# Starting the first scan of a Mamba layer: order of the first two pieces, dt in halves, input loads spread over the scans

## The chip, the cores and the metric

The kernel runs on one core of one Trainium2 chip. The metric is the device time of one execution in microseconds (us); the time before is the median of three runs. One execution was also recorded by the hardware profiler; all traces in this document are of such executions. Engines: PE does matrix products, ACT activation functions, DVE and POOL elementwise work (DVE also the scan instruction), SP issues the DMAs.

## The reference

Four layers run one after the other on an image of 2 x 256 x 48 x 48 floats. Only the first, a Mamba layer, is touched by the change. Per batch image it has 2304 tokens of 256 channels:

```
h   = layernorm(seq) + pos                       # pos: table of sines and cosines, scaled
xi, z = split(h @ in_proj.T)                     # 512 channels each
# for the forward direction, and once more with xi and z reversed in time:
xs  = silu(causal_conv4(xi) + conv_b)
dt, B, C = split(xs @ xproj.T)                   # 16, 16 and 16 columns
dt  = softplus(dt @ dtproj.T + dt_b)
state[t] = exp(dt[t] * A) * state[t-1] + dt[t] * xs[t] * B[t]     # 16 states a channel
y[t]  = sum_n state[t] * C[t] + D * xs[t]
out = seq + ((y_f * silu(z)) + (y_b * silu(z))) @ out_proj.T
```

The other layers (attention with a feed-forward part, a graph layer with experts, attention with a mixture of experts) follow and read what the first one left.

## The kernel before, in words

**Tiling.** Each image is cut into 6 pieces of W = 384 tokens. Channels lie on the 128 partitions: 256 channels are two blocks, the 512 inner channels DB = 4 blocks, so a whole tile of inner channels is 128 x 1536. The input x stays in SBUF as `xres` (L73) for the whole kernel. Every float32 matmul shows in the trace as two matmul instructions.

**Three kinds of work per piece**, each a Python generator that yields between its steps so that its instructions can be laid between those of another:

- `project_in(b, c)` (L213): load pos; layer norm through matmuls with a constant matrix (means L221, difference L222, square L224, variance L228, Sqrt L230, scalings of pos L232, reciprocal L236, products L238 and L240); then eight output blocks, L247 with copy L252, of which the first four (xi) go to DRAM at L254 and the last four (z) at L256. It has 12 steps: 4 of normalization, 8 of blocks.
- `prepare(b, s, c, got)` (L297): load the window xw of xi from DRAM (L302), convolution as matmuls with diagonal weights (L311, copies L315), Silu (L321), xproj (L327, L331; B and C go to DRAM, L333), then dt: four small matmuls (L341) with Abs and Relu (L344, L345), and softplus on whole 128 x 1536 tiles: Exp L347, plus one L350, Ln L352, minus one L353, three DVE steps L355 to L357, and on POOL dtu = dt * xs (L359).
- `scan(step, beside, ...)` (L499): for each of the 4 channel blocks and 16 states one decay (ACT, L544), one scan instruction (DVE, L550 forward, L553 backward) and one product with C (L558, on DVE or POOL), summed by PE (L512). POOL makes the inputs db of four states at a time (L527) from bb, which with cc is loaded from DRAM for each group of four states (L522, L524). Two states make a slot; a scan has 32.

**Order.** There are 24 scans: two images, two directions, six pieces. During scan i, `beside` holds the generators that are laid into its slots: `prepare` for scan i+1 (15 steps over 25 slots), and during the first ten scans `project_in` for pieces (0, 2) to (1, 5), one per scan (12 steps over 32 slots). Before the first scan, `project_in(0, 0)`, `project_in(0, 1)` and `prepare(0, "f", 0)` run one after the other in the Python text. The eleven loads of x beyond the first (L167) are issued ahead of all that, and the 1 MB weight w_in in one DMA (L199).

The Python order isn't the order on the chip. The framework places each instruction on its engine's queue by its own estimate of when it is ready: earlier text goes first, but a later instruction is taken forward where the estimate sees the engine idle. On the chip each engine then works its queue strictly in that order, SP's DMA issues included. The framework also inserts all waits. Buffers are shared by tag: `up` has one buffer per tag (h, sq, pos, rs, xw, ex, ln), `wp` two (xs, dt, dtu, xz, bb, cc, db); the tag ln also serves the backward scans' yf (L504). PSUM tiles come from `hold()` (L208): five buffers before the scans begin, one during them.

Of the kernel before, what the change touches and what calls it, by code (L numbers as in the profile page):

```python
# [18 lines left out]
F32 = mybir.dt.float32  # L19
I32 = mybir.dt.int32  # L20
BF16 = mybir.dt.bfloat16
AF = mybir.ActivationFunctionType
ALU = mybir.AluOpType
# [4 lines left out]
P = 128  # L28
NB, C, HH, WW = 2, 256, 48, 48
L = HH * WW  # L30
T = NB * L
NT = T // P
W = 384
NCH = L // W
# [64 lines left out]
def bc(ap, shape, axis):  # L99

    return ap.unsqueeze(axis).to_broadcast(shape)
# [60 lines left out]
    yield  # L162


def load_x(E, b, c):
    xin = E.p["x"].rearrange("b (k p) n -> p b k n", p=P)
    E.nc.sync.dma_start(  # L167
        E.xres[:, :, b * L + c * W : b * L + (c + 1) * W], xin[:, b, :, c * W : (c + 1) * W]
    )

# [1 line left out]
def layer0(ctx, E):  # L174
# [9 lines left out]
    nc, tc, p = E.nc, E.tc, E.p  # L184
    NS, DB = 16, 4
# [5 lines left out]
    wp = ctx.enter_context(tc.tile_pool(name="l0w", bufs=2))  # L191
    up = ctx.enter_context(tc.tile_pool(name="l0u", bufs=1))
    psh = ctx.enter_context(tc.tile_pool(name="l0ps_h", bufs=5, space=PSUM))
    ps = ctx.enter_context(tc.tile_pool(name="l0ps_s", bufs=1, space=PSUM))
    psy = ctx.enter_context(tc.tile_pool(name="l0ps_y", bufs=1, space=PSUM))

    load_x(E, 0, 0)
    w_in = big.tile([P, 2, 1024], F32, name="w_in")
    nc.sync.dma_start(w_in, p["in_proj_wT"].rearrange("(k p) m -> p k m", p=P))  # L199
    xi_d, z_d, yf_d = [], [], []  # L200
    edge = up.tile([P, DB, 3], F32, name="edge")
    nc.vector.memset(edge, 0.0)
# [5 lines left out]
    def hold():  # L208

        pool, tag = (ps, "mm") if scanning else (psh, "hs")  # L210
        return pool.tile([P, 512], F32, tag=tag, name="mm")[:, :W]

    def project_in(b, c):  # L213

        src = E.xres[:, :, b * L + c * W : b * L + (c + 1) * W]
        pos = up.tile([P, 2, W], F32, tag="pos", name="pos")
        nc.sync.dma_start(pos, p["pos"].rearrange("(k p) n -> p k n", p=P)[:, :, c * W : (c + 1) * W])
        h = up.tile([P, 2, W], F32, tag="h", name="h")
        mp = hold()
        for k in range(2):  # L220
            nc.tensor.matmul(mp, lhsT=E.mean_c, rhs=src[:, k, :], start=k == 0, stop=k == 1)  # L221
        nc.vector.tensor_tensor(h, src, bc(mp, [P, 2, W], 1), ALU.subtract)  # L222
        sq = up.tile([P, 2, W], F32, tag="sq", name="sq")
        nc.scalar.activation(sq, h, AF.Square)  # L224
        yield
        vp = hold()
        for k in range(2):
            nc.tensor.matmul(vp, lhsT=E.mean_c, rhs=sq[:, k, :], start=k == 0, stop=k == 1)  # L228
        rs = up.tile([P, 2 * C], F32, tag="rs", name="rs")[:, :W]
        nc.scalar.activation(rs, vp, AF.Sqrt, bias=E.eps[1e-5])  # L230
        for k in range(2):
            nc.scalar.activation(  # L232
                pos[:, k, :], pos[:, k, :], AF.Identity, bias=E.v("ln_b", k, 1), scale=E.v("pos_scale")
            )
        yield
        nc.vector.reciprocal(rs, rs)  # L236
        yield
        nc.vector.tensor_tensor(h, h, bc(rs, [P, 2, W], 1), ALU.mult)  # L238
        for k in range(2):
            nc.vector.scalar_tensor_tensor(  # L240
                h[:, k, :], h[:, k, :], E.v("ln_g", k, 1), pos[:, k, :], ALU.mult, ALU.add
            )
        yield
        for m in range(2 * DB):
            px = hold()
            for k in range(2):
                nc.tensor.matmul(  # L247
                    px, lhsT=w_in[:, k, m * P : (m + 1) * P], rhs=h[:, k, :],
                    start=k == 0, stop=k == 1,
                )  # L250
            xz = wp.tile([P, W], F32, tag="xz", name="xz")
            nc.scalar.copy(xz, px)  # L252
            if m < DB:
                nc.sync.dma_start(xi_d[b][:, m, 3 + c * W : 3 + (c + 1) * W], xz)  # L254
            else:
                nc.sync.dma_start(z_d[b][:, c, m - DB], xz)  # L256
            yield

    scanning = False
    first = project_in(0, 0)  # L260
    next(first)
    for b in range(NB):
        for c in range(NCH):
            if (b, c) != (0, 0):
                load_x(E, b, c)
        nc.sync.dma_start(xi_d[b][:, :, 0:3], edge)
        nc.sync.dma_start(xi_d[b][:, :, L + 3 : L + 6], edge)
    w_x, w_dt, nega, w_d = {}, {}, {}, {}
# [14 lines left out]
    one = big.tile([P, 2], F32, name="one")  # L283
# [10 lines left out]
            nc.scalar.activation(t[:, j, :], E.ident, AF.Copy, scale=E.v(f"conv_w_{s}", j, 1))  # L294
        return t

    def prepare(b, s, c, got):  # L297

        fwd = s == "f"
        t0 = c * W  # L300
        xw = up.tile([P, DB, W + 3], F32, tag="xw", name="xw")
        nc.sync.dma_start(xw, xi_d[b][:, :, t0 + (0 if fwd else 3) : t0 + W + (3 if fwd else 6)])  # L302
        if (b, s) not in w_cv:
            w_cv[b, s] = taps(s)
        yield
        xs = wp.tile([P, DB, W], F32, tag="xs", name="xs")
        for d in range(DB):
            px = hold()
            for k in range(4):
                o = k if fwd else 3 - k  # L310
                nc.tensor.matmul(  # L311
                    px, lhsT=w_cv[b, s][:, d * 4 + k, :], rhs=xw[:, d, o : o + W],
                    start=k == 0, stop=k == 3,
                )
            nc.scalar.activation(xs[:, d, :], px, AF.Identity, bias=E.v(f"conv_b_{s}", d, 1))  # L315
            if d == 0:
                y = wp.tile([P, DB, W], F32, tag="y", name="y")
                if not fwd:
                    nc.sync.dma_start(y, z_d[b][:, c])
            yield  # L320
        nc.scalar.activation(xs, xs, AF.Silu)  # L321
        if not fwd:
            nc.scalar.activation(y, y, AF.Silu)
        yield
        pj = hold()
        for d in range(DB):
            nc.tensor.matmul(  # L327
                pj[:48, :], lhsT=w_x[s][:, d, :], rhs=xs[:, d, :], start=d == 0, stop=d == DB - 1
            )
        pr = wp.tile([48, W], F32, tag="pr", name="pr")  # L330
        nc.scalar.copy(pr, pj[:48, :])  # L331
        bcd = dr.tile([48, W], F32, tag="bcd", name="bcd")
        nc.sync.dma_start(bcd[16:48, :], pr[16:48, :])  # L333
        yield


        dt = wp.tile([P, DB, W], F32, tag="dt", name="dt")
        ex = up.tile([P, DB, W], F32, tag="ex", name="ex")
        for d in range(DB):
            pd = hold()  # L340
            nc.tensor.matmul(  # L341
                pd, lhsT=w_dt[s][:, d * P : (d + 1) * P], rhs=pr[0:16, :], start=True, stop=True
            )
            nc.scalar.activation(ex[:, d, :], pd, AF.Abs, bias=E.v(f"dt_b_{s}", d, 1))  # L344
            nc.scalar.activation(dt[:, d, :], pd, AF.Relu, bias=E.v(f"dt_b_{s}", d, 1))  # L345
            yield
        nc.scalar.activation(ex, ex, AF.Exp, scale=-1.0)  # L347
        dtu = wp.tile([P, DB, W], F32, tag="dtu", name="dtu")
        ln = up.tile([P, DB, W], F32, tag="ln", name="ln")
        nc.scalar.activation(dtu, ex, AF.Identity, bias=one[:, 0:1])  # L350
        yield
        nc.scalar.activation(ln, dtu, AF.Ln)  # L352
        nc.scalar.activation(dtu, dtu, AF.Identity, bias=one[:, 1:2])  # L353
        yield
        nc.vector.tensor_tensor(ex, ex, dtu, ALU.subtract)  # L355
        nc.vector.tensor_tensor(dt, dt, ln, ALU.add)
        nc.vector.tensor_tensor(dt, dt, ex, ALU.add)  # L357
        yield
        nc.gpsimd.tensor_tensor(dtu, dt, xs, ALU.mult)  # L359
        got.extend((b, s, c, xs, y, dt, dtu, bcd))  # L360
        yield

    def project_out(b, c, y):

# [216 lines left out]
    order = [  # L581
        (b, s, i, i if s == "f" else NCH - 1 - i) for b in range(NB) for s in "fb" for i in range(NCH)
    ]
    for steps in (first, project_in(0, 1)):
        for _ in steps:
            pass
    ready = []
    for _ in prepare(0, "f", 0, ready):
        pass
    scanning = True  # L590
    pieces = [(0, c) for c in range(2, NCH)] + [(1, c) for c in range(NCH)]
    after = None
    heads = chain(head_products(), contexts())
    n_late = -(-(36 + 1 + 2 * 5 * NCH) // (len(order) - 1 - len(pieces)))
    for i, (b, s, step, c) in enumerate(order):
        now, ready = ready, []
        beside = [(after, 4, 8)] if after else []
        if i + 1 < len(order):
            nb, s2, _, c2 = order[i + 1]
            beside.append((prepare(nb, s2, c2, ready), 15, 25))  # L600
        if i < len(pieces):
            beside.append((project_in(*pieces[i]), 12, 32))
        elif len(pieces) <= i < len(order) - 1:

            beside.append((islice(heads, n_late), n_late, 32))
        if (b, s, step) == (1, "f", 1):

            beside.append((group_stats(E, up, lambda: hold()[:, 0:2], 0), 3, 20))
        scan(step, beside, *now)
        after = chain(project_out(b, c, now[4]), piece_stats(E, b, c)) if s == "b" else None  # L610
# [1522 lines left out]
```

## Time and profile before

| what | us |
|---|---|
| median of 3 runs (5334.69 to 5339.48) | 5338.1 |
| the profiled execution | 5298.49 |
| its span | 5296.7 |
| first matmul of the first piece's blocks (L247) | 20.14 |
| first scan instruction (L550) | 102.11 |
| last PE sums of the last scan (L512) begin | 2457.18 |
| DVE busy over the span | 3472.5 |
| POOL busy over the span | 2416.0 |
| ACT busy over the span | 2395.3 |
| PE busy over the span | 4765.0 |

A row of the timeline gives start, length, engine, line, operation, what is written from what, and in brackets how long the engine was idle before it and what released it. "SPq" is SP's queue: the time is that of issuing, not of the transfer. A busy PE is not a PE at its peak, since matmul ends are modelled.

### The profile page before, as it was taken

How to read it: one execution, taken by the hardware profiler on the slowest of the kernel's cores; microseconds unless marked ns; L12 is line 12 of the kernel's file. 1: busy time of each engine (PE TensorE's matmuls, PEld its weight loads, DVE VectorE, ACT ScalarE, POOL GpSimd, SP SyncE). 2: the span in 40 equal slices, each digit the busy share in tenths (PEclk: the TensorE clock that was granted, in tenths of full speed). 3: DMA queues.
4: the chain of work that ended last, by engine and by line, in shares of the span. 5: the costliest groups of instructions: out<-in, count | busy, mean ns of one | idle time of the engine just before them, and what ended most of it. 6: DMA issues, size and time to landing. Idle time of an engine off the chain costs nothing. (4 is left out here: it accounts for less than half of the span.)

```text
span 5296.7 us, 47498 instructions
## 1 busy us (share of the span) xinstructions
PE 4765.0 (90%) x15282; PEld 2642.2 (50%) x15282; DVE 3472.5 (66%) x5366; ACT 2395.3 (45%) x5021; POOL 2416.0 (46%) x1323
## 2 busy tenths in 40 slices
PE   7888888888888888877999999999999999999897
PEld 3444344444444434433555555556655555555676
DVE  4999988889888878889999544546724410211344
ACT  5767766765766766762222323422133222222221
POOL 2888887788888788886000000028612100000331
PEclk8999999999999999999999999999989999999898
DMA  4454454444544344443110000111121100000422
GB/s 155 167 173 172 169 177 159 167 173 165 173 150 161 138 162 152 162 152 135 36 44 32 6 16 1 38 33 28 19 96 48 48 3 9 7 9 6 85 84 97
DMA packets 187427, 504.63 MB, mean 95 GB/s; under 512 B 33591, under 2 KB 106683, under 8 KB 186908
## 3 DMA queue, kind: packets, MB, share of 16 engines
q1 hardware_dynamic: 178460, 488.74, 26.9%
q0 software_dynamic: 8704, 12.73, 1.6%
q8 instruction: 123, 2.02, 0.2%
q14 instruction: 140, 1.15, 0.1%
HBM read 425.88 MB, written 75.51 MB: 95 GB/s over the span
## 5 line engine op out<-in xcount | busy, mean ns | idle before, releaser
L512 PE MATMUL yp<-hc,ident 128*128 128x384 f32 x3072 | 1185.8, 517 | 206.3 <-DVE hc L558 166.1
L527 POOL TENSOR_TENSOR db<-dtu,bb 128x1536 f32<-128x1536 f32 x384 | 1322.9, 3445 | 53.5 <-DVE hs L553 13.5
L512 PEld LDWEIGHTS yp<-hc,ident 128*128 128x128 f32 x3072 | 573.4, 197 | 764.5 <-DVE hc L558 317.7
L558 POOL TENSOR_TENSOR hc<-ho,cc 128x384 f32<-128x384 f32 x576 | 587.9, 1028 | 243.6 <-DVE ho L553 103.1
L558 DVE TENSOR_TENSOR hc<-hs,cc 128x384 f32<-128x384 f32 x960 | 499.9, 538 | 82.5 <-PE yp L512 81.3
L544 ACT ACTIVATE hs<-dt,negab 128x384 f32<-128x384 f32 x768 | 435.2, 581 | 94.6 <-DVE hc L558 44.1
L544 ACT ACTIVATE hs<-dt,negaf 128x384 f32<-128x384 f32 x768 | 434.5, 581 | 67.3 <-DVE hc L558 32.6
L550 DVE TENSOR_TENSOR_SCAN hs<-hs,state,db 128x384 f32<-128x384 f32 x400 | 395.3, 1008 | 33.9 <-POOL db L527 21.5
L553 DVE TENSOR_TENSOR_SCAN hs<-hs,state,db 128x384 f32<-128x384 f32 x400 | 393.3, 1005 | 34.6 <-POOL db L527 16.1
L1938 POOL DMA_INDIRECT xe<-xt_d,token x48 | 47.4, 987 | 752.5 <-issue 713.1
L311 PE MATMUL mm<-xw,w_cv 128*128 128x384 f32 x768 | 287.5, 517 | 56.6 <-ACT xs L315 17.9
L1873 PE MATMUL po<-at,xtok 128*128 128x384 f32 x864 | 329.5, 506 | 8.2 <-ACT at L1871 8.1
L1864 PE MATMUL sp<-qT,xn 128*128 128x384 f32 x864 | 317.2, 486 | 0.0
L1871 ACT ACTIVATE at<-sp 128x384 f32<-128x384 f32 x216 | 104.8, 491 | 467.2 <-PE sp L1864 467.1
L1511 PE MATMUL ph<-xn,w 128*128 128x384 f32 x768 | 288.9, 519 | 17.7 <-ACT hid L1515 6.0
L1069 POOL PARTITION_ALL_REDUCE most<-most x1 | 0.4, 381 | 629.5 <-PE tp L939 629.5
L800 PE MATMUL pf<-t,wfc 128*128 128x384 f32 x768 | 256.0, 488 | 3.5 <-ACT hid L804 2.7
L819 PE MATMUL po<-hid,wfc 128*128 128x384 f32 x768 | 253.7, 486 | 0.0
L553 DVE TENSOR_TENSOR_SCAN ho<-hs,state,db 128x384 f32<-128x384 f32 x240 | 239.2, 997 | 14.4 <-ACT hs L544 14.3
L550 DVE TENSOR_TENSOR_SCAN ho<-hs,state,db 128x384 f32<-128x384 f32 x240 | 239.0, 996 | 8.7 <-ACT hs L544 8.7
L560 ACT COPY state<-hs 128x1 f32<-128x1 f32 x800 | 117.6, 155 | 277.5 <-DVE hc L558 274.6
L1515 ACT ACTIVATE hid<-ph,vec 128x384 f32<-128x384 f32 x192 | 110.6, 581 | 292.8 <-PE ph L1511 259.2
(465 smaller groups left out, 8022.8 us busy)
## 6 DMA issues: line engine op xcount, KB each, us to landing
bb<-bcd SPq DMA_DIRECT2D x192, 768.0 KB, 4.2
cc<-bcd SPq DMA_DIRECT2D x192, 768.0 KB, 4.1
xw<-xi_d SPq DMA_DIRECT2D x24, 774.0 KB, 5.8
w<-in_m_w SPq DMA_DIRECT2D x16, 1024.0 KB, 5.8
y_d<-y SPq DMA_DIRECT2D x32, 384.0 KB, 2.3
ye<-y_d SPq DMA_DIRECT2D x32, 384.0 KB, 3.4
xi_d<-xz SPq DMA_DIRECT2D x48, 192.0 KB, 2.3
z_d<-xz SPq DMA_DIRECT2D x48, 192.0 KB, 3.2
```

Source lines behind the costliest of these rows:

```text
L311: nc.tensor.matmul(px, lhsT=w_cv[b, s][:, d * 4 + k, :], rhs=xw[:, d, o : o + W], start=k == 0, stop=k == 3,)
L512: nc.tensor.matmul(yp[d], lhsT=E.ident, rhs=hc, start=False, stop=summed[d] == NS)
L527: nc.gpsimd.tensor_tensor(db, bc(dtu[:, d, :], [P, GN, W], 1), bb, ALU.mult)
L544: nc.scalar.activation(hs, dt[:, d, :], AF.Exp, scale=nega[s][:, d * NS + n : d * NS + n + 1])
L550: nc.vector.tensor_tensor_scan(to, hs, db[:, j], init, ALU.mult, ALU.add)
L553: nc.vector.tensor_tensor_scan(to[:, ::-1], hs[:, ::-1], db[:, j, ::-1], init, ALU.mult, ALU.add)
L558: (nc.gpsimd if on_pool else nc.vector).tensor_tensor(hc, to, cc[:, j, :], ALU.mult)
L800: nc.tensor.matmul(pf, lhsT=wfc1[:, k, f * P : (f + 1) * P], rhs=t1[:, k, :], start=k == 0, stop=k == 1,)
L819: nc.tensor.matmul(po[m], lhsT=wfc2[:, f, m * P : (m + 1) * P], rhs=hid[:, i, :], start=f == 0, stop=f == 15,)
L1511: nc.tensor.matmul(ph, lhsT=w1[:, e, k, f * P : (f + 1) * P], rhs=xn[:, k, c * W : (c + 1) * W], start=k == 0, stop=k == 1,)
L1864: nc.tensor.matmul(sp, lhsT=xn[:, k, t0 + i * P : t0 + (i + 1) * P], rhs=qT[:, k, c * W : (c + 1) * W], start=k == 0, stop=k == 1,)
L1873: nc.tensor.matmul(po[m], lhsT=xtok[:, i, m * P : (m + 1) * P], rhs=at, start=i == 0, stop=i == MT - 1,)
```

## The change

- `load_x` takes an optional tile `after`: a DVE copy of one element per partition and block from it into the destination comes first, so that the load waits for it.
- w_in is loaded in two halves: the columns of xi before everything, those of z after the first piece's xi blocks.
- Of the x pieces only (0, 0), (0, 1) and (0, 2) are loaded before the scans. During scan i the piece of scan i+1's `project_in` is loaded, with the dt tile of scan i as `after`; that makes nine such loads.
- Before the scans: seven more steps of the first projection (to its fourth xi block), then `prepare` of the first scan step by step; from its sixth step (Silu) on, two steps of `fill` after each. `fill` is what is left of the first projection (four z blocks), then the whole projection of the second piece.
- `prepare` has `parts`. With 2, as for the first scan, dt is made in two halves of two channel blocks, each with its own Exp, Ln, DVE and POOL steps; the tiles are handed over after the first half. The second half's six steps lie in the first six slots of scan 0. With 1, its steps are those of before; the tiles dtu and ln are asked for ahead of the dt blocks.

```diff
-def load_x(E, b, c):
+def load_x(E, b, c, after=None):
     xin = E.p["x"].rearrange("b (k p) n -> p b k n", p=P)
-    E.nc.sync.dma_start(
-        E.xres[:, :, b * L + c * W : b * L + (c + 1) * W], xin[:, b, :, c * W : (c + 1) * W]
-    )
+    dst = E.xres[:, :, b * L + c * W : b * L + (c + 1) * W]
+    if after is not None:
+        E.nc.vector.tensor_copy(dst[:, :, 0:1], after[:, 0:2, 0:1])
+    E.nc.sync.dma_start(dst, xin[:, b, :, c * W : (c + 1) * W])
...
-    nc.sync.dma_start(w_in, p["in_proj_wT"].rearrange("(k p) m -> p k m", p=P))
+    in_wT = p["in_proj_wT"].rearrange("(k p) m -> p k m", p=P)
+    nc.sync.dma_start(w_in[:, :, :512], in_wT[:, :, :512])
...
     for b in range(NB):
-        for c in range(NCH):
-            if (b, c) != (0, 0):
-                load_x(E, b, c)
         nc.sync.dma_start(xi_d[b][:, :, 0:3], edge)
...
-    def prepare(b, s, c, got):
+    def prepare(b, s, c, got, parts=1):
...
+        n = DB // parts
+        for d0 in range(0, DB, n):
+            ds = slice(d0, d0 + n)
+            for d in range(d0, d0 + n):
+                pd = hold()
+                nc.tensor.matmul(
+                    pd, lhsT=w_dt[s][:, d * P : (d + 1) * P], rhs=pr[0:16, :], start=True, stop=True
+                )
+                nc.scalar.activation(ex[:, d, :], pd, AF.Abs, bias=E.v(f"dt_b_{s}", d, 1))
+                nc.scalar.activation(dt[:, d, :], pd, AF.Relu, bias=E.v(f"dt_b_{s}", d, 1))
+                yield
+            nc.scalar.activation(ex[:, ds], ex[:, ds], AF.Exp, scale=-1.0)
+            nc.scalar.activation(dtu[:, ds], ex[:, ds], AF.Identity, bias=one[:, 0:1])
             yield
...
+            nc.scalar.activation(ln[:, ds], dtu[:, ds], AF.Ln)
+            nc.scalar.activation(dtu[:, ds], dtu[:, ds], AF.Identity, bias=one[:, 1:2])
+            yield
+            nc.vector.tensor_tensor(ex[:, ds], ex[:, ds], dtu[:, ds], ALU.subtract)
+            nc.vector.tensor_tensor(dt[:, ds], dt[:, ds], ln[:, ds], ALU.add)
+            nc.vector.tensor_tensor(dt[:, ds], dt[:, ds], ex[:, ds], ALU.add)
+            yield
+            nc.gpsimd.tensor_tensor(dtu[:, ds], dt[:, ds], xs[:, ds], ALU.mult)
+            if d0 == 0:
+                got.extend((b, s, c, xs, y, dt, dtu, bcd))
+            yield
...
-    for steps in (first, project_in(0, 1)):
-        for _ in steps:
-            pass
+    load_x(E, 0, 1)
+    for _ in islice(first, 7):
+        pass
+    nc.sync.dma_start(w_in[:, :, 512:], in_wT[:, :, 512:])
+    load_x(E, 0, 2)
     ready = []
-    for _ in prepare(0, "f", 0, ready):
+    head = prepare(0, "f", 0, ready, 2)
+    fill = chain(first, project_in(0, 1))
+    n = 0
+    while not ready:
+        next(head)
+        n += 1
+        if n > 5:
+            for _ in islice(fill, 2):
+                pass
+    for _ in fill:
         pass
...
         beside = [(after, 4, 8)] if after else []
+        if i == 0:
+            beside.append((head, 6, 6))
+        if i + 1 < len(pieces):
+            load_x(E, *pieces[i + 1], after=now[5])
```

More of the change, by code (lines that the diff above doesn't have):

```diff
@@ L337, in prepare @@
         dt = wp.tile([P, DB, W], F32, tag="dt", name="dt")
+        dtu = wp.tile([P, DB, W], F32, tag="dtu", name="dtu")
         ex = up.tile([P, DB, W], F32, tag="ex", name="ex")
[L339 to L345, printed above, removed]
-            yield
@@ L347, in prepare @@
[L347 to L361, printed above, removed]
+        ln = up.tile([P, DB, W], F32, tag="ln", name="ln")
+        n = DB // parts
[11 more added lines that the diff above has]
+            nc.scalar.activation(dtu[:, ds], ex[:, ds], AF.Identity, bias=one[:, 0:1])
+            yield
+            nc.scalar.activation(ln[:, ds], dtu[:, ds], AF.Ln)
[9 more added lines that the diff above has]
+            yield
```

## Prediction

> **What bounds the kernel now.** I read the page first. Its slices show three stages; only the first two matter here.
>
> ```profile
> span 5296.7 us, 47498 instructions
> DVE  4999988889888878889999544546724410211344
> POOL 2888887788888788886000000028612100000331
> ```
>
> A slice is 132 us. In the first one VectorE (DVE) is busy 4 tenths and GpSimd (POOL) 2; from the second on, through the 24 scans, both are at 8 to 9. So there is a start in which the two scan engines hardly work, and then a stage that they bound. The chain that ended last reaches back only into late PE work, so for the start I asked for busy time by stretch (columns: stretch and length, then PE, PEld, DVE, ACT, POOL, granted PE clock, DMA share, GB/s).
>
> ```profile
> 34.00:43.00 9.00, 2.30 (x7) 0.80 (x5) 5.01 (x5) 2.17 (x4) 0.00 (x0) 0.99 0.46 160
> 43.00:55.00 12.00, 11.88 (x32) 6.98 (x33) 0.60 (x2) 3.67 (x8) 0.00 (x0) 0.87 0.34 116
> 66.00:102.00 36.00, 23.22 (x56) 10.53 (x56) 9.57 (x7) 26.38 (x32) 7.00 (x2) 0.89 0.35 122
> 102.00:200.00 98.00, 79.77 (x202) 37.86 (x203) 88.03 (x119) 65.54 (x170) 90.02 (x46) 0.90 0.48 161
> 200.00:300.00 100.00, 83.08 (x237) 41.53 (x236) 93.00 (x118) 71.79 (x175) 86.74 (x44) 1.00 0.49 171
> ```
>
> DVE is 90 to 93% busy once scans run: an early start is worth its full length only if no DVE work moves into the scans. Then the timeline of the start (start, length, engine, line, operation, count, idle before it):
>
> ```profile
> 31.45 0.59 SPq L302 DMA_DIRECT2D xw<-xi_d  x1
> 33.29 1.45 PE L221 MATMUL mm<-xres,mean_c 128*128 128x384 f32 x4
> 43.12 12.08 PE L247 MATMUL mm<-h,w_in 128*128 128x384 f32 x32 [4.91 <-DVE h L240]
> 55.04 10.49 PE L311 MATMUL mm<-xw,w_cv 128*128 128x384 f32 x32
> 67.47 1.48 ACT L321 ACTIVATE xs<-xs 128x1536 f32<-128x1536 f32 x1
> 69.00 4.34 PE L327 MATMUL mm<-xs,w_xf 128*48 128x384 f32 x8 [3.47 <-ACT xs L321]
> 80.34 1.48 ACT L347 ACTIVATE ex<-ex 128x1536 f32<-128x1536 f32 x1
> 86.97 1.48 ACT L352 ACTIVATE ln<-dtu 128x1536 f32<-128x1536 f32 x1
> 93.02 1.75 DVE L357 TENSOR_TENSOR dt<-dt,ex 128x1536 f32<-128x1536 f32 x1
> 94.92 3.66 POOL L359 TENSOR_TENSOR dtu<-dt,xs 128x1536 f32<-128x1536 f32 x1 [85.02 <-DVE dt L357]
> 102.11 0.96 DVE L550 TENSOR_TENSOR_SCAN hs<-hs,db 128x384 f32<-128x384 f32 x1 [6.82 <-POOL db L527]
> ```
>
> The first scan starts at 102.11. Its window xw was asked for at 31.45 and takes 5.3 us to land (DMA issues of the start), so the convolution L311 could run at 37; it runs at 55.04, because PE's order puts the second piece's L247 ahead, which itself waits for that piece's normalization. These 18 us are the first target. The second is 67 to 102: one chain through ACT, DVE and POOL on whole 128x1536 tiles. Scans end near 2459, so (2459-102)/24 = 98 us each.
>
> **The change, part by part.**
>
> *Convolution ahead of the second piece.* L247 of the first piece starts at 20.14. The loads of x in front of it get fewer; the square L224 starts at 10.47 though h was ready at 8.8, behind the pos scalings, and L228 at 12.42 though sq was ready at 11.3, behind a second piece's mean: 0 to 2.8 us to win, I take 1. The four xi blocks are 16 matmul instructions, 8 at the 0.64 us step seen at 20 to 25 us and 8 at the later 0.32: 7.7. Copy 0.48, store 2.4, issue and landing of xw 5.7. Sum: 19.1+7.7+0.5+2.4+5.7 = 35.4. Convolution 10.5 plus a copy 0.6: 46.5. Table load 1.28 and Silu 1.48: 49.3. L327 took 4.34, half of it at the 0.64 step after 3.5 us of an idle PE; with the second piece's matmuls in that gap I take 3, plus 0.47: 52.8.
>
> *dt in halves.* Two blocks instead of four: wait 1.3 and four activations 2.0, to 56.1. Half tiles by the row of the 128x768 square (0.83): Exp with table load 2.1, Identity 0.85, Ln with load 2.1, Identity 0.85: 62.0. Two DVE steps of 0.95 (row: h L222): 63.9. POOL half: between 1.03 (128x384) and 3.44 (128x1536), by their line 1.8: 65.7; first db 3.44: 69.2.
>
> *The fill.* The second piece still has to be done before the scans: ACT work of two pos scalings 1.3, square 0.84, Sqrt 0.58, 12 copies 5.7 and perhaps two table loads. About half finds room while PE convolves (ACT was busy 4.16 of 11 us there), half stands in the chain: 0 to 10 us, I take 4.5. First scan at 74 (69 to 79): **28 us earlier** (23 to 33).
>
> *What is given back in scan 0.* The second dt half's DVE work comes in: 3 x 0.95 = 2.9. In the trace the third piece's normalization (L222 at 55.24, L236 at 85.69, and L238, L240: 5.7 us of DVE) was already done in the idle time ahead of the scans; with less idle time half to all of it slides into scan 0: 2.9 to 5.7, I take 3.5. ACT has 8 us of second half plus convolution copies and a Silu which ran early before; ACT at 66 to 72% has 28 us to spare over a scan, but not in its first 18 us: waits of 0 to 8, I take 3, with POOL's extra 1.8 ahead of a db in it (POOL is above 90% there). Together 9.4 (5.8 to 17).
>
> Here the skill speaks against halves. ScalarE: Activation LUTs, "What ACT_TABLE_LOAD costs", charges 2.66 us for each switch, drain included. The trace has 1.28, and the next activation begins 0.01 later (205.33 load, 206.62 Sqrt). The split adds two loads in scan 0 (Ln, back to Exp) and maybe two in the start: 2.6 to 5.1 by the trace, 5.3 to 10.6 by the page, which would push the start 2 to 3 us later. I go by the trace.
>
> *w_in in halves, x loads one per scan.* The first w_in half waits for the same mask work (issue 10.55 before) and lands well before 19. Nine loads go into scans, each behind a DVE copy of two elements per partition, never seen in the trace; the nearest row is ACT's 128x1 copy at 0.16: 9 x 0.16 = 1.4, not below zero since DVE gains nothing by it. Dearer could be the wait that it adds on SP: behind a load that waits for DVE stand bb and cc of the coming groups, and POOL's db and hc behind those. DMA: Bandwidth & Descriptors, "Anatomy of one DMA — SWDGE (gpsimd) path", says that a semaphore wait is made on the issuing sequencer before dispatch, so everything behind is held. The trace shows the like (columns: total, times, longest):
>
> ```profile
> SPq L522 <- POOL db L527: 698.0, 174, 13.6
> SPq L524 <- DVE hc L558: 654.9, 143, 17.5
> SPq L505 <- DVE dt L356: 47.5, 9, 8.5
> ```
>
> A load that waited for DVE held SP 47.5/9 = 5.3 us. By the rule alone nine would cost up to 47 us. But SP stands in such waits for most of the stage, and among POOL's releasers over 200 to 2400 us no DMA appears: bb and cc always landed first. The copy reads dt, which was made some 30 us before its scan (dtu of the second scan at 167.67, scans 98 us apart from 102). So 0 to 47, and I take the near end, 0. The bytes, 9 x 384 KB, add 4 GB/s to 170. The tiles dtu and ln are now asked for before the dt blocks instead of behind Exp; their first writers (L350, L352) stand where they stood, so I take 0; if ln's buffer, shared with yf in backward scans, held something longer, the row L505 above is the price, once a backward scan.
>
> **Sum.** 28 - 9.4 - 1.4 = 17 us. The profiled execution (5298.5 us, span 5296.7) would go to 5281. The timed runs' median is 5338.1, 40 us above the profiled one, and I assume that the difference doesn't touch the start: 5338 - 17 = 5321. The later stages start as the last scan ends (DVE goes to L1023 at 2457.51), so the shift should carry to the end.
>
> One reservation holds for all of it: the instruction order isn't Python's but comes from the framework's own estimate. Backward scans in the trace come at distances of 96 to 108 us, so a new order could move the 24 scans together by some 8 us either way.
>
> **Rivals.**
> - *Borrowed start* (same). The idle DVE time was in use: all 5.7 us slide into scan 0, ACT is late for its first groups, and the fill stands in the chain: 23 - 17 - 1.4 = 5, to 5333. For it: the row at 66 to 102 shows DVE 9.57 and ACT 26.38 busy. Against: the 29.49 us of DVE idle time before L236 at 85.69. The same figure comes if the change doesn't do what it says because the order again puts the second piece's L247 ahead of L311: then only the halves gain, about 9 on the ACT chain, less 2.9 and 1.4.
> - *Loads hold SP* (slower). Place: each x load on SP ahead of bb, cc. Price: 5.3 us x 9 = 47 if all reaches POOL, to 5368; at half of it 5345. It decides from 17/9 = 1.9 us per load on, and makes slower from (17+10.7)/9 = 3.1. For it: queue order. Against: no POOL wait on DMA in 2200 us.
> - *More* (faster). Chain undisturbed, 69, and the third piece still early: 33 - 5.8 - 1.4 = 26, to 5312; with a luckier order 5304.
>
> **Numbers.** Measurement can tell about 0.2%, 10.7 us, from no change. Forecast (a gain of 11 to 24) 0.46; more than that 0.14; borrowed start or no new order 0.22; loads hold SP, or a worse order of the scans, 0.18. So faster 0.60, same 0.22, slower 0.18. Range 5304 to 5346: the better order at one end, half of the SP price at the other.
>
> **What would show it.** Right: L311 starts near 35 to 38, ahead of the second piece's L247; L347 and L352 in 128x768; the first L550 near 74; DVE above 90% at once, dtu of scan 1 some 70 us later; last scans near 2442. Wrong: L311 still after 50; the distance of dtu L359 over the first six scans above 98 (it is 96.6); POOL waits on bb or cc; SPq L167 waits on DVE of several us each.

## Result and the profile after

The changed kernel took 5363.77 us (six runs, 5353.56 to 5368.84) where the kernel before took 5338.79 (six runs): ratio 1.0043, 95% interval 1.0033 to 1.0052. It is 25 us slower, and 5321 was predicted.

The page of the changed kernel, its span and the slices of the two scan engines:

```profile
span 5365.9 us, 47548 instructions
DVE  4899989888888888889999445456534400211344
POOL 3788887777888788785000000048402100000331
```

The digits hardly show the loss. VectorE falls from 9 tenths to 8 in the second slice, but that is 119.4 us busy in a slice of 132.4 against 118.2 in one of 134.2; in the first slice it gains only 7 us of work (54.5 to 61.8), though the scans start 23 us earlier. The two spans are not compared with each other: the last scan begins 22 us later than before, and the other 47 us between the profiled executions arise in later layers, which the change leaves alone. The kernel before alone had medians of 5290.6, 5292.7, 5299.5 and 5338.1 us on the chips of the four groups of runs below, so only ratios to it on the same chip are used. The traces come from different chips too.

Timeline of the start (start, length, engine, line, operation, count, idle before it and its releaser):

```profile
32.67 13.29 PE L313 MATMUL mm<-xw,w_cv 128*128 128x384 f32 x32 [7.83 <-DMA xw<-xi_d]
64.26 0.84 ACT L354 ACTIVATE ex<-ex 128x768 f32<-128x768 f32 x1
66.30 13.55 PE L251 MATMUL mm<-h,w_in 128*128 128x384 f32 x32 [3.05 <-DVE h L244]
67.39 0.84 ACT L357 ACTIVATE ln<-dtu 128x768 f32<-128x768 f32 x1
70.22 0.96 DVE L362 TENSOR_TENSOR dt<-dt,ex 128x768 f32<-128x768 f32 x1
79.11 0.97 DVE L556 TENSOR_TENSOR_SCAN hs<-hs,db 128x384 f32<-128x384 f32 x1 [7.73 <-ACT hs L550]
```

The convolution (L313) is ahead of the second piece's blocks (L251), the halves are there, and the first scan starts at 79.1 where it started at 102.1: the start did what it was meant to. The next rows show what came of it (columns of the windows: stretch, length, then PE, PEld, DVE, ACT, POOL, granted PE clock, DMA share, GB/s; first the kernel after, then before, each over its first scan).

```profile
79.00:89.00 10.00, 1.91 (x6) 0.65 (x4) 3.54 (x5) 3.12 (x9) 2.01 (x2) 0.68 0.54 145
79.00:198.00 119.00, 89.18 (x227) 42.88 (x225) 96.21 (x116) 79.82 (x184) 85.81 (x43) 0.90 0.43 146
```

```profile
102.00:191.00 89.00, 71.88 (x178) 33.39 (x178) 79.03 (x107) 59.28 (x152) 81.02 (x41) 0.89 0.47 160
```

The first scan lasts 119 us and not 89: VectorE works 17 us more in it and stands idle 13 us more, most of that in the first ten microseconds, where it works 3.54. So the second scan starts at 198.1, 7 us later than before, with the whole gain of the start gone. In both traces, cut where each scan's first scan instruction stands (us):

| | first scan starts | scan 0 | scans 1-5 | 6-8 | 9-11 | 12-22 | last scan starts |
|---|---|---|---|---|---|---|---|
| before | 102.1 | 89.2 | 484.4 | 312.7 | 301.3 | 1086.6 | 2376.3 |
| after | 79.1 | 118.9 | 487.7 | 316.2 | 313.2 | 1083.3 | 2398.5 |

Three questions follow: why scan 0 gives back 30 us, what the copies ahead of the loads cost, and where the rest of scans 1 to 11 comes from.

### The profile page after: what moved, and what is told of

It reads as the page before. It is cut to its first block, busy times and chain, and to the rows that moved or that the text cites. A ratio compares the mean times of both kernels' runs of the same rounds, so it can differ in the third digit from the quotient of the medians.

```text
span 5365.9 us, 47548 instructions
## 1 busy us (share of the span) xinstructions
PE 4782.7 (89%) x15282; PEld 2651.0 (49%) x15282; DVE 3491.4 (65%) x5378; ACT 2401.4 (45%) x5029; POOL 2416.9 (45%) x1324
## 5 line engine op out<-in xcount | busy, mean ns | idle before, releaser
L564 POOL TENSOR_TENSOR hc<-ho,cc 128x384 f32<-128x384 f32 x576 | 588.6, 1028 | 268.7 <-DVE ho L559 96.6
L550 ACT ACTIVATE hs<-dt,negaf 128x384 f32<-128x384 f32 x768 | 434.7, 582 | 66.5 <-DVE hc L564 32.7
L313 PE MATMUL mm<-xw,w_cv 128*128 128x384 f32 x768 | 295.6, 529 | 68.0 <-ACT state L566 18.5
L313 PEld LDWEIGHTS mm<-xw,w_cv 128*128 128x128 f32 x768 | 151.7, 204 | 200.4 <-ACT state L566 29.3
```

Of the source, the lines that this page charges most:

```text
L313: nc.tensor.matmul(px, lhsT=w_cv[b, s][:, d * 4 + k, :], rhs=xw[:, d, o : o + W], start=k == 0, stop=k == 3,)
L550: nc.scalar.activation(hs, dt[:, d, :], AF.Exp, scale=nega[s][:, d * NS + n : d * NS + n + 1])
L564: (nc.gpsimd if on_pool else nc.vector).tensor_tensor(hc, to, cc[:, j, :], ALU.mult)
```

## Experiments

### The start alone, the loads alone

Theory: the start is worth nothing, since the work only moves, and the loads make the loss. Rivals: SP's waits, or the start itself. First the changed kernel with all loads of x put back ahead of everything, as before (called e1 from here on), and none left in the scans:

```diff
-        if i + 1 < len(pieces):
-            load_x(E, *pieces[i + 1], after=now[5])
```

> The changed kernel with all eleven x loads issued at the start again, as before the change; no DVE copy is left. Theory A (three prices: the start gains 23 us and scan 0 gives 25 of them back; the nine DVE copies cost 13 us because a copy is held while POOL works; with them the order of scans 6 to 8 changes, another 10): last scan 2 us later than before, 5341, first scan near 79. Rival B (start and halves are the whole loss, the loads cost nothing): 5362. Rival C (the loads hold SP): 5341 as well, so this run separates only A and C from B.

Measured: 1.0002 (0.9994 to 1.0011). Then the kernel before with only the loads moved, each behind its copy (e2):

```diff
+        if i + 1 < len(pieces):
+            load_x(E, *pieces[i + 1], after=now[5])
```

> The kernel before with only the loads changed: x one piece per scan behind its DVE copy, start and dt as before. Theory A: copies 13 us and the order of scans 6 to 8 another 10: 5360, with copies of up to 4.4 us in the trace. Rival B: 5339, no change. Rival C (SP is held): 5360, and POOL waits on bb or cc in the trace.

Measured: 1.0035 (1.0023 to 1.0047). Together they make 1.0037 of the 1.0043: the loads with their copies carry the loss, and the new start brings neither gain nor loss. In the third, the changed kernel keeps its loads but makes the copy on ACT:

```diff
-        E.nc.vector.tensor_copy(dst[:, :, 0:1], after[:, 0:2, 0:1])
+        E.nc.scalar.copy(dst[:, :, 0:1], after[:, 0:2, 0:1])
```

> The changed kernel with the two-element copy ahead of each x load made by ACT instead of DVE; SP's load still waits for an engine's copy. Theory A: the price of the copies falls to 9 x 0.2 us and the DVE order of scans 6 to 8 is that of before: 5342. Rival C (it is the wait on SP): stays near 5364. Rival B (start and halves): 5362.

Measured: 1.0006 (0.9999 to 1.0012). The loads still stand on SP and still wait for dt; only the engine of the copy differs. So SP's waits are not the price: it is VectorE's copy. (VectorE's order of work from scan 1 on is then that of before as well, so this run doesn't part a copy's own time from what it does to the order.)

### What a copy costs

The nine copies of the changed kernel, with the least, middle and largest duration in ns, the first and last start:

```profile
L171 DVE COPY xres<-dt x9: 169/806/4416, 71.2 to 895.8; 128x2 f32<-128x2 f32 x9
```

Two elements per partition take up to 4.4 us; the nine together take 13.4 us. The timeline shows with what they end:

```profile
294.32 1.00 POOL L564 TENSOR_TENSOR hc<-ho,cc 128x384 f32<-128x384 f32 x1 [0.19 <-DVE ho L556]
294.54 0.81 DVE L171 COPY xres<-dt 128x2 f32<-128x2 f32 x1
295.26 1.01 DVE L556 TENSOR_TENSOR_SCAN hs<-hs,state,db 128x384 f32<-128x384 f32 x1
295.28 3.44 POOL L533 TENSOR_TENSOR db<-dtu,bb 128x1536 f32<-128x1536 f32 x1
```

The copy ends (295.35) as POOL's hc ends (295.32). Each of the eight long ones ends within 0.04 us of the end of the POOL instruction beside it, whereas the first, 0.17 us at 71.2, has POOL beside it only in its last 0.05 us. The two longest, 4.39 and 4.42 us, outlast a whole db (3.44): in each, POOL goes on from an hc to the next hc and then to a db before the copy ends. The scan instruction runs on beside a whole db; its hs lies in PSUM, so that db is its one input from SBUF. This is what the Trainium skill states in SBUF — State Buffer, "Who interferes with whom": a VectorE copy that runs in a two-port mode (both of VectorE's SBUF ports at work on one tensor), or an instruction with two inputs in SBUF, and a GpSimd instruction that reads SBUF exclude one another for a whole instruction, and a VectorE instruction with one input from SBUF, outside that mode, stays out of it. In which mode the copy ran, no trace shows. I had not weighed that page. To test it, the copy in e2 was made in two other ways: as a maximum of two inputs (e6) and as a reciprocal, which has one input (its result is overwritten by the load).

```diff
-        E.nc.vector.tensor_copy(dst[:, :, 0:1], after[:, 0:2, 0:1])
+        E.nc.vector.tensor_tensor(dst[:, :, 0:1], after[:, 0:2, 0:1], after[:, 0:2, 0:1], ALU.max)
...
+        E.nc.vector.reciprocal(dst[:, :, 0:1], after[:, 0:2, 0:1])
```

> e2 (before, with the loads per scan), its DVE copy replaced by a DVE maximum of the same two elements with themselves: same place, same wait for SP, another kind of DVE instruction. If the copies were long because this kind of instruction can't run beside a POOL operation: 0.1 to 0.2 us each instead of up to 4.4, and the ratio falls from 1.0035 to about 1.0015, which is left for the order of scans 6 to 8. If they were long for where they stand (or any DVE instruction there is held): still 0.8 to 4.4 us and 1.0035.

> e2 (before, with the loads per scan), its DVE copy replaced by a DVE reciprocal of the same two elements (their values are overwritten by the load). L236, a reciprocal with one input, is the one DVE instruction of the scans that never took longer beside POOL in any trace here (2.54 to 2.55), while the copy and the two-input maximum of e6 ended with POOL's operation. If what holds the copies is a port that such an instruction doesn't need: 0.1 to 0.3 us each, and the ratio falls from 1.0035 to 1.001 or less. If held as well, or if the order of scans 6 to 8 carries the loss: 1.0035.

Measured: 1.0038 (1.0027 to 1.0050) and 1.0018 (1.0012 to 1.0025). Their rows:

```profile
L171 DVE TENSOR_TENSOR xres<-dt x9: 333/802/4404, 94.3 to 889.3; 128x2 f32<-128x2 f32 x9
```

```profile
L171 DVE RECIPROCAL xres<-dt x9: 150/157/160, 94.6 to 882.6; 128x2 f32<-128x2 f32 x9
```

The two-input form is held like the copy, the reciprocal never. The rule agrees with this case. But the reciprocal still loses 0.0018, so being held is not the whole price. (Nine reciprocals change VectorE's order too, in scans 1 to 3 and 6 to 8.) Next, the kernel before with nine such copies into a tile that nothing reads, and its loads where they were:

```diff
+        if i + 1 < len(pieces):
+            nc.vector.tensor_copy(scrap, now[5][:, 0:2, 0:1])
```

> The kernel before with nothing but nine two-element DVE copies added, from the scan's dt into a scrap tile at the place of the per-scan loads; all loads of x at the start, as before. If the loss of e2 is the copies': 1.0025 to 1.0035 with no load moved. If it is the loads (SP, contention): 1.000.

Measured: 1.0028 (1.0017 to 1.0039), with 16.5 us of copies. No loads moved, and most of the loss is there.

### Held time or a new order

A marker also changes what the framework makes of the order: with the nine copies, VectorE's order differs from that of before in scans 4, 5, 7 and 8 (with the loads moved, in 6 too). Copies at scans 4, 7 and 8 alone do that; copies at scans 0, 1, 2, 3, 5 and 6 alone leave it as it was. So the edit above was made at these six scans alone, then with `i in (4, 7, 8)`, and then with a reciprocal in place of the copy at those three:

```diff
+        if i in (0, 1, 2, 3, 5, 6):
+            nc.vector.tensor_copy(scrap, now[5][:, 0:2, 0:1])
```

> The kernel before with a copy of two elements per partition from dt into an unused tile at the start of scans 0, 1, 2, 3, 5 and 6. With just these six, VectorE's order of work in all 24 scans stays that of the kernel before. Nine such copies cost 1.0028. Theory that the time the copies are held behind GpSimd is the cost: the six took 3.4, 4.4 and four times 0.8 or more, about 11 us, so 1.002. Rival, that the changed order of scans 6 to 8 is the cost: nothing of it is left, so at most 1.0003.

> The same with copies at scans 4, 7 and 8 only, the three that change VectorE's order in scans 4, 7 and 8. Held-copy theory: 0.8, 0.3 and up to 4.4 us, together 2 to 6 us, so 1.0003 to 1.0011. Order theory: 1.0018 or more, as with the nine reciprocals.

> As the run with three copies at scans 4, 7 and 8, but with a reciprocal in the copy's place: the order changes in the same scans 7 and 8, and none is held (0.16 us each). Held-copy theory: 1.0000 to 1.0002. Order theory: 1.0018. If the run lies at 1.0018 and the one with six copies at 1.0002, the held time is not what is paid.

| | markers | their time, us | order | ratio |
|---|---|---|---|---|
| six copies | scans 0-3, 5, 6 | 10.99 | as before | 1.0018 (1.0011 to 1.0024) |
| three copies | 4, 7, 8 | 5.54 | new | 1.0017 (1.0010 to 1.0025) |
| three reciprocals | 4, 7, 8 | 0.45 | new | 1.0017 (1.0010 to 1.0024) |

Neither theory is enough alone. The six copies cost 10.4 us with the order as before (difference of the medians; the interval allows 5.8 to 12.7), and the three reciprocals 10.3 with nothing held.

What held time costs is better read from the traces, scan by scan: in the seven kernels with no marker on VectorE and the order of before, each of the scans 1 to 5 has the same length within 0.2 us. With the six copies, the one of 4.39 us at the end of scan 0 makes that scan 93.6 us long and not 89.2; those of 0.80 in scans 1 and 2 make 97.2 of 96.5; scan 3, without one, takes 96.5 as before. Over scans 0 to 5 it is 6.5 us for 7.6 us held, so there held time is paid nearly in full. The other 3.4 of the 11.0 us lie ahead of the first scan, where VectorE is idle anyway. The three copies hold 5 us more than the reciprocals at the same ratio; the two intervals, 3.7 us to either side, leave room for that.

How markers that are not held cost time shows later in the scans. In the traces it isn't scans 7 and 8 that are longer (before 211.6 us, with the three reciprocals 209.6) but scans 9 to 11, whose order of work is the same. In scan 11, with the reciprocals and then before:

```profile
1192.00:1299.00 107.00, 94.81 (x257) 50.94 (x258) 91.33 (x122) 55.70 (x91) 82.10 (x42) 0.86 0.43 150
```

```profile
1190.00:1289.00 99.00, 85.89 (x256) 45.35 (x256) 90.66 (x121) 54.60 (x89) 81.22 (x42) 0.95 0.47 163
```

The same 256 or so matmuls take PE 94.8 us and not 85.9, at a granted clock of 0.86 and not 0.95. Scans 6 to 11 take 614 us in the trace of before and 610 to 614 in those of six others, 616 to 619 in three, and 624 to 629 in the changed kernel's and in those of six others; both ends occur among kernels whose VectorE order is that of before from scan 1 on. The traces' records of the granted clock tell more. In all 17 traces the clock is full or half, and it changes only on a grid of 3.41 us steps (every change lies within 0.01 us of it). Where on this grid scan 11 begins goes with its length in every trace, whatever the kernel:

| scan 11 begins, us after a step of the grid | traces | steps at half clock | PE busy, us | scan 11, us |
|---|---|---|---|---|
| 0.28 to 0.94 | before and six others | 3 to 5 | 85.9 to 89.0 | 99.1 to 101.2 |
| 2.82 to 2.96 | after, three reciprocals and five others | 9 to 10 | 94.7 to 96.6 | 106.5 to 109.2 |
| 3.15 to 3.25 | three copies and two others | 4 | 87.3 to 87.8 | 99.6 to 100.0 |

By an estimate from these figures, five more steps at half clock take up to 5 x 1.7 = 8.5 us of PE's work; PE is busy some 7 us longer, and the scan is 7 us longer. So a marker that shifts a scan by a fraction of a microsecond may cost or save 7 us there. No run sets the start of scan 11 on purpose; this is read from the traces as they fell.

Over the timed runs of this group the mean clock was 0.9659 for before, 0.9636 with six copies and 0.9627 with three reciprocals. A line fitted to the 54 executions of before falls by 2.8 us for each 0.001 of mean clock. By this estimate the lower clock goes with 6.5 of the 9.3 us that the six copies cost (difference of the means) and with all of the reciprocals' 8.8. In the same way it goes with some 13 of the 17 us of e2 (0.9602 against 0.9651). Why kernels with markers get the lower clock more often, no run shows.

### Where scan 0 gives it back

What releases VectorE in scan 0 of the changed kernel (total, times, longest):

```profile
DVE hs L556 <- ACT hs L550: 11.6, 3, 7.7
DVE ho L556 <- ACT hs L550: 6.3, 1, 6.3
```

It waits for ACT's decays. The 7.7 is the wait ahead of the first scan instruction itself, so that inside scan 0 they make 10.2 of 22.7 us of idle time; the rest is spread over POOL's db (4.0), ACT's Ln (3.8) and others. The timeline tells what ACT waits for:

```profile
80.06 0.32 SPq L528 DMA_DIRECT2D bb<-bcd  x1
80.47 0.86 SPq L258 DMA_DIRECT2D xi_d<-xz  x2
85.86 0.48 ACT L256 COPY xz<-mm 128x384 f32<-128x384 f32 x1 [6.85 <-DMA xi_d<-xz]
86.37 0.58 ACT L550 ACTIVATE hs<-dt,negaf 128x384 f32<-128x384 f32 x1
86.99 0.96 DVE L556 TENSOR_TENSOR_SCAN ho<-hs,db 128x384 f32<-128x384 f32 x1 [6.32 <-ACT hs L550]
101.08 3.21 DVE L361 TENSOR_TENSOR dt<-dt,ln 128x768 f32<-128x768 f32 x1 [0.53 <-ACT ln L357]
```

The second piece's blocks now run on into the scan. The tag xz has two buffers; ACT's next copy into one (L256) needs the store of the last (L258) to be done. On SP the store stands behind the load of bb for a coming group, which goes out only at 80.06, as the scan lets its buffer go; from the stores' issue at 80.47 it is another 5.4 us until ACT goes on. So ACT is stuck for 6.85 us, and the decays behind that copy with it. The last row is VectorE's work that moved in: the second half of dt, whose step with two inputs is held for 3.21 us (0.96 in the start).

Three kernels attack this, all with the loads of x early, so that their base is the 1.0002. In one, the fill begins with the first step:

```diff
-        if n > 5:
+        if n > 0:
```

> As e1, and the fill (two steps of the rest of the first and of the second piece's projection) starts after the first step of the first preparation instead of its sixth, so that the second piece's stores stand on SP ahead of scan 0's bb and cc. Theory A (scan 0 pays because ACT waits for an xz buffer whose store stands behind a bb load): first scan at 75 to 80, scan 0 near 100 instead of 115 us, last scan 10 to 14 earlier than before: 5327. Rival D (borrowed start: scan 0 lacks DVE and ACT time for the work that slides in, whatever the order): 5339 to 5343.

Measured: 0.9996 (0.9988 to 1.0004). In one (e5) the second piece's blocks get four-block tiles that the start doesn't use yet (the edit below, for that piece only), so that no copy waits for a store; in a third dt is made whole on top of that:

```diff
-            xz = wp.tile([P, W], F32, tag="xz", name="xz")
+            if m % DB == 0:
+                four = wp.tile([P, DB, W], F32, tag="xs" if m < DB else "y", name="four")
+            xz = four[:, m % DB, :]
```

> As e1 (x loads at the start), and the second piece's eight blocks are copied into two tiles of their own instead of the two turning xz buffers, so ACT never waits for a store that stands on SP behind scan 0's bb. Theory A: ACT's wait of 6.9 us on xi_d<-xz is gone and DVE's 12 us of extra idle time in scan 0 with it; first scan near 79, scan 1 starts at 182 to 186 instead of 194 (e1) and 191 (before); ratio to before 0.9985. Rival D (borrowed start: DVE's idle time moves, whatever is done): scan 1 at 191 to 194, ratio 1.000.

> As e5 with dt of the first scan made whole, as before the change; the fill's place is the changed kernel's. Theory A: the chain before the first scan is 8 to 9 us longer (first scan near 88), scan 0 is 3 us of DVE work shorter; scan 1 starts 5 us later than in e5, ratio 0.9995. Rival (halves bring nothing, since what they save comes back in scan 0): as e5.

Measured: 1.0009 (1.0000 to 1.0018) and 1.0001 (0.9992 to 1.0010). With buffers of its own the stall at 80 is gone and another takes its place (same kernel, dt in halves):

```profile
94.17 0.96 DVE L564 TENSOR_TENSOR_SCAN hs<-hs,db 128x384 f32<-128x384 f32 x1 [0.74 <-ACT hs L558]
95.24 0.56 DVE L572 TENSOR_TENSOR hc<-hs,cc 128x384 f32<-128x384 f32 x1
103.79 0.96 DVE L369 TENSOR_TENSOR dt<-dt,ln 128x768 f32<-128x768 f32 x1 [7.99 <-ACT ln L365]
```

ACT's Ln for the second half stands there behind the first convolution copy of the second scan, which waits for PE, which waits for that scan's window, which waits for the stores of the second piece. So the second scan's preparation was moved back, in the kernel with its own buffers, by 8 slots (e11) and by 12:

```diff
-            beside.append((prepare(nb, s2, c2, ready), 15, 25))
+            coming = prepare(nb, s2, c2, ready)
+            beside.append((coming, 15, 25) if i else (chain(iter([None] * 8), coming), 23, 28))
```

> As e5 (x at the start, own buffers for the second piece's blocks), and the second scan's preparation begins eight slots later in scan 0, so that its convolution, which needs the second piece's stores, no longer stands early on ACT and PE. Theory A: e5's 8 us of DVE idle time at 95 to 104 is gone, scan 1 starts at 183 to 186 (before: 191), ratio 0.9985. Rival D: the wait turns up at a third place, scan 1 at 190 or later, ratio 1.000.

> As e11 with twelve slots instead of eight, spread to the thirtieth. Theory A: as e11 within 2 us, unless the preparation then ends too late for scan 1, which would show as DVE idle time at the head of scan 1. Rival D: 1.000.

Measured: 0.9999 (0.9990 to 1.0007) and 1.0009 (1.0000 to 1.0018). Last, dt of the first scan in halves alone, in the kernel before:

```diff
-    for _ in prepare(0, "f", 0, ready):
-        pass
+    head = prepare(0, "f", 0, ready, 2)
+    while not ready:
+        next(head)
```

> The kernel before with only dt of the first scan in halves; order of the two pieces, loads and weights as before. Theory A: first scan at 94 instead of 102, scan 0 3 to 5 us longer: 4 us gained, ratio 0.9993. Rival D: scan 1 starts at 191 as before, 1.000.

Measured: 1.0009 (1.0000 to 1.0018). What each did to the start (us; VectorE's idle time is that ahead of the first scan plus that in scan 0):

| | first scan | its length | DVE busy in it | DVE idle | second scan |
|---|---|---|---|---|---|
| before | 102.1 | 89.2 | 79.4 | 76.4 + 9.9 | 191.3 |
| after | 79.1 | 118.9 | 96.3 | 61.0 + 22.7 | 198.1 |
| after, early loads | 80.7 | 113.6 | 91.8 | 62.7 + 21.8 | 194.3 |
| fill from first step | 90.1 | 101.8 | 91.4 | 71.2 + 10.4 | 191.9 |
| own buffers | 84.2 | 109.2 | 89.6 | 66.3 + 19.5 | 193.4 |
| own buffers, whole dt | 98.3 | 97.4 | 85.4 | 76.9 + 12.0 | 195.7 |
| 8 slots later | 81.0 | 103.8 | 93.0 | 63.0 + 10.8 | 184.8 |
| 12 slots later | 80.4 | 112.9 | 93.6 | 62.5 + 19.2 | 193.3 |
| before, halves | 89.0 | 101.8 | 91.5 | 70.2 + 10.4 | 190.8 |

First scans from 79 to 102 all lead to a second scan at 191 to 198, but for one. The two idle times of a row add up to 81 to 89 us in all rows except with 8 slots, where it is 74: an earlier first scan buys idle time inside the scan. So ACT's wait for its buffer was only one of several waits, and theory A's ratios of 0.9985 were not met. With 8 slots both stalls are gone and the second scan does come 6.5 us early, but scan 1 then takes 99.4 us and not 96.5, nearly all of it new idle time, and at scan 6 the lead is 3.3 us (672.4 against 675.7). That would be 0.9994, which the interval can't tell from nothing, and single traces vary by more later on (scans 6 to 11 by 13 us).

## Why the prediction was wrong

- **Start 28 us earlier (23 to 33).** Right within its range: 23.0. Convolution at 32.7 (35.4), first scan at 79.1 (74): from convolution to scan it took 46.4 us where the sum had 38.6, 2.8 of it because the convolution took 13.3 and not 10.5, the rest because the fill's share of the chain was larger than the 4.5 taken. The table loads that the halves add were 1.28 us each in the start and in scan 0, and the next activation began 0.01 or 0.02 later, so the trace's figure was the right one to take against the 2.66 of ScalarE: Activation LUTs, "What ACT_TABLE_LOAD costs".
- **"Together 9.4 (5.8 to 17)" given back in scan 0.** This step failed: 29.7, of which the copy is 4.4. DVE's busy time grew by 16.9. That is 4.4 for the copy, and 12.5 against the 6.4 that I took (2.9 for the half of dt and 3.5 for the third piece's normalization): all of that normalization slid in and took 7.5 us there, not 5.7, and dt's half took 5.1. In each a step with two inputs was held beside POOL (2.85 and 3.21 us where 0.96 was taken). Idle time grew by 12.8 where I took 3. I counted ACT's work there, but not the stores that the fill issues on SP, behind the scan's own loads, nor the two xz buffers that tie ACT to them. That is not all of it either: with own buffers the idle time in scan 0 was still 19.5 us, as other waits took the place of this one.
- **"9 x 0.16 = 1.4" for the copies.** This step failed too: the nine lasted 13.4 us in the trace, and the loads with their copies cost 0.0035, 18.6 us, of which by the estimate above some 13 go with a lower clock. I took the duration from an ACT row for a VectorE instruction, though the two engines differ in just what decides: ACT's copies took 0.18 to 0.20 us each at the same places. The range had no room for it. By the Trainium skill's page SBUF — State Buffer, "Who interferes with whom", each copy is open to the rest of a POOL instruction, up to 3.4 us by the row of db (two took 4.4), and the windows shown with the prediction have POOL busy for 87 to 92% of the first two scans. The trace of before had the sign of it too, in a product of two SBUF tiles that took 0.96 us in the start and mostly 2.7 beside the scans' POOL work:

```profile
L238 DVE TENSOR_TENSOR h<-h,rs x9: 944/2691/2791, 216.1 to 1018.7; 128x768 f32<-128x768 f32 x9
```

- **SP's waits at 0 (of 0 to 47).** Right. The loads behind ACT's copies cost at most 0.0012, and the loss is there with no load moved. The slower rival had the right sign and the wrong mechanism.
- **"A new order could move the 24 scans together by some 8 us either way."** Named as a reservation and left out of the sum; three reciprocals that change it cost 10.3 us. By the estimate above this goes with a lower clock, which in scan 11 depends on where the scan begins on the clock's grid; why it is lower more often with the markers stays open.
- **Borrowed start.** This rival was right for the start part: 1.0002, at a price in scan 0 even above its own 17 us.

The sum that the runs give: start 0.0002, loads with copies 0.0035, together 0.0037, which lies in the interval of the measured 1.0043. In the trace the last scan starts 22.2 us late: the start gives -23.0, scan 0 +29.7, scans 1 to 5 +3.3, scans 6 to 8 +3.5, scans 9 to 11 +11.9 and the rest -3.3. No version that was run beats the kernel before beyond its interval; the nearest, the fill from the first step, stands at 0.9996.

## What to carry to other kernels

An instruction that only marks an order is not free on a busy engine: price it by a row of the same engine beside the same neighbours, and put it where no one contends (here ACT); a form that is not held, as the reciprocal here, is not free by that alone. Before a loss of 0.2% is put down to an instruction, compare the mean clock of the runs. When work is laid into another stage's waits, follow each of its stores and loads through the queue that they share with that stage, and the buffers that these hold. If the engine that bounds the next stage has its idle time filled by nothing new, an early start only moves idle time: count what that engine must still do before the second stage ends.

## What the hardware showed that I had not expected

- A copy of 2 elements per partition on VectorE took 0.33 to 4.42 us beside a busy POOL and 0.17 with next to none beside it; a two-input maximum of the same size 0.33 to 4.40; a reciprocal 0.15 to 0.16 at the same places.
- The granted PE clock was full or half, and changed only on a grid of 3.41 us steps. Scan 11, with the same order of work in all 17 traces, took 106.5 to 109.2 us where it began 2.82 to 2.96 us after a step, and 99.1 to 101.2 where it began anywhere else that a trace shows.
